# An RK4 scan with two quantized feed-forwards: a searched order of issue, a norm's shift pre-written in PSUM, and merged scale operations

## The chip, the cores and the metric

The kernel runs on one core of one Trainium2 chip, in one launch. The metric is the device time of that launch in microseconds; the time before is 832.3 us, the median of three runs (832.07 to 835.12). The core has five engines that each work through a queue of their own in order: PE (matrix products), DVE, ACT and POOL (elementwise work, called VectorE, ScalarE and GpSimd elsewhere), and SP, which issues DMAs.

## The reference, cut to what matters

The input `x` has 128 sequences of 32 time steps of 256 numbers, `cond` has 128 x 256. Two layers follow each other, each with a first part and a feed-forward (all in float32):

```python
# layer 0, first part: 32 steps of Runge-Kutta 4 over the state (q, p), driven by x[:, t, :]
dq = q - q**3 / 3 - p + drive + tanh(q) @ coupling.T + bias
dp = 0.08 * (q + 0.7 - 0.8 * p)              # four slopes a step, q and p clipped to +-20
# layer 0, feed-forward on the q of every step, with block quantization (blocks of 32):
#   scale = 2**floor(log2(max |block|)), elements rounded to a few bits, clipped
x = x + q_act(silu(q_act(q) @ wg.T) * (q_act(q) @ wu.T)) @ wd.T
# layer 1, first part: modulated norm, then attention with 16 heads over the 32 steps
scale, shift = split(cond @ W_emb + b_emb)
xn = rms_norm(x, g_norm) * (1 + scale) + shift
o = attention(rms_norm(q), rms_norm(k), v)   # qkv = xn @ W_qkv
h = o + o @ W_out
# layer 1, feed-forward: Hadamard rotation, 8-bit rows, ternary weights
x = x + h_bitlinear(silu(h_bitlinear(h, wg)) * h_bitlinear(h, wu), wd)
```

## The kernel before, in words

The batch of 128 lies on the 128 partitions. Stage one goes over the 32 time steps: `step` computes one Runge-Kutta step, and `ffn0` takes the state of that step through layer 0's feed-forward and layer 1's norm and writes the normalized row, turned, into `xnT`. Stage two goes over 32 groups of 128 tokens (4 sequences of 32 steps): `tokens` computes attention and layer 1's feed-forward. The PSUM buffers of the two stages are different, and the first group of stage two waits for all 32 `xnT` copies.

No engine's order is written by hand. Every piece of work is an `Item` given to `Work.add`, with its engine, a cost in microseconds, the buffers that it reads and writes, a rank, and marks such as `port` (the planner lets no two items with that mark run at once on DVE and POOL). `Work.order` simulates the items with these costs, forth and back in time in turn, 40 times, with the priorities taken from the times of the pass before, and keeps the order with the earliest modelled end; stage by stage. The items are then issued in that order, each engine's own part of it as its queue. `keep_warm` adds empty matmuls (L1367) where the plan has gaps on PE.

What the change and the prediction touch:

- `mx_scales` (L679, L684, L691): three DVE instructions on the maxima of the blocks. L679 scales the maxima from an SBUF tile (`amax`) into a small PSUM tile (`top`); L684 and L691 read `top`, cut out the exponent bits as int32, and leave the scale `scl` and its inverse `inv` in SBUF. `ffn0` calls it twice a step: for 8 blocks of the state and for 32 blocks of the inner row. `mx_weight` calls it six times, for the weights; there L736 multiplies `scl` once more, in SBUF.
- Behind these, L922 (DVE) or L970 (POOL) multiplies by `inv`, L902 clips, and L928 or L978 (POOL) multiplies by `scl`. L629 is POOL's multiplication in the four slopes of the Runge-Kutta step, L573 DVE's multiply and add there, L665 its clipping. L740, L752 and L761 are POOL's work on the weights.
- The norm at the end of `ffn0`: L985 (ACT) writes x into `ps_po`, a single PSUM slot, and eight matmuls (L989) add the down product; ACT copies the sum out (L995) and takes its squares (L1001), POOL the inverse root (L1006, L1007). For the first 27 steps ACT scales (L1012) and POOL multiplies by `gain` (L1016) and adds `shift` (L1020); for the last five (`LATE`) DVE does both (L1025, L1027). PE turns the row into a slot of `ps_turn` (L547) and ACT copies it into `xnT` (L1030).
- `modulation` computes `gain` and `shift` once, early.
- In stage two L1253 is two DVE instructions on one element per partition, the scales of gate and up. L1091, L1092 and L1323 are more small scale instructions. L1104 is a DVE instruction on 32 int32 numbers in `rsqrt` (a multiply and an add, SBUF to SBUF) between POOL's instructions L1101 and L1112. L1307 are the butterflies of the rotation, on POOL and DVE, and L1173 POOL's multiplication of the queries by their gains.

Of the kernel before, what the change touches and what calls it, by code (L numbers as in the profile page):

```python
# [13 lines left out]
I32 = mybir.dt.int32  # L14
# [56 lines left out]
class Buf:  # L71


    def __init__(self, slots):
        self.slots, self.slot = slots, None
        self.writers, self.readers, self.left = [], [], 0
        self.end, self.fixed, self.pool = 0.0, False, None
# [6 lines left out]
class Slot:  # L84
    def __init__(self, ap, bank=None):
        self.ap, self.bank, self.free = ap, bank, 0.0


class Item:


    def __init__(self, engine, cost, fn, rank, table, port, tail, records):
        self.engine, self.cost, self.fn, self.rank = engine, cost, fn, rank
        self.table, self.port, self.tail, self.records = table, port, tail, records
        self.after, self.before, self.open = [], [], 0
        self.bufs, self.outs, self.small, self.behind, self.warm = [], (), False, (), None
        self.ready, self.start, self.end = 0.0, None, None


class Work:  # L100

    TAIL = {PE: 0.165, DVE: 0.085, ACT: 0.1, POOL: 0.045, SP: 0.0}
# [7 lines left out]
    ROUNDS = 40  # L112
    GAP, SECOND = 0.45, 100.0

# [3 lines left out]
    def add(  # L118
# [16 lines left out]
        for b in item.bufs:  # L135
            b.left += 1
# [3 lines left out]

    def start_of(self, item, now, port, table):
        t = max(now, item.ready)
        if not self.strict and not all(i in self.gone for i in item.behind):
            return math.inf
        if item.port:
            t = max(t, port)
        for b in item.bufs:
            if b.slots and b.slot is None:
                free = [s.free for s in b.slots if s.free < math.inf]
                if self.strict and b not in b.pool[: len(free)]:  # L150
                    return math.inf
                t = max(t, min(free, default=math.inf))
        if item.table and item.table != table:
            t += self.LOAD
        last = self.last[item.engine]
        if item.engine == PE:
            t = max(t, self.fetched(item.records) - item.cost)
            if last and last.small != item.small:
                t = max(t, now + self.COLD)
        elif item.engine == DVE and last and self.banks(last.outs) & self.banks(item.bufs):  # L160
            t = max(t, now + self.WITHIN[DVE])
        return t

    @staticmethod
    def banks(bufs):
        return {b.slots[b.slot or 0].bank for b in bufs if b.slots} - {None}

    def fetched(self, n):

        n -= self.BLOCK  # L170
        for records, t in reversed(self.issued):
            n += records
            if n > 0:
                return t + self.FETCH
        return 0.0
# [7 lines left out]
    def run(self, items, forth, before):  # L183

        ready = {e: [] for e in (PE, DVE, ACT, POOL, SP)}  # L190
        now = dict.fromkeys(ready, 3.0 if forth else 0.0)
        if forth:
            now[POOL] = 7.0
        port, table = 0.0, None
        self.issued, self.last, self.gone = [], dict.fromkeys(ready), set(before)
        for item in items:
            item.open = 0
            item.ready = 0.0
            for a in item.after if forth else item.before:
                if a in self.gone:  # L200
                    item.ready = max(item.ready, a.end + self.gap(a, item))
                elif (a.rank < self.SECOND) == (item.rank < self.SECOND):
                    item.open += 1
            for b in item.bufs:
                b.left, b.end = 0, 0.0
                if b.slots and not b.fixed:
                    b.slot = None
                for s in b.slots:
                    s.free = 0.0
        if forth:  # L210
            for item in before:
                now[item.engine] = max(now[item.engine], item.end)
                self.last[item.engine] = item
                table = item.table or table
                for b in item.bufs:
                    for s in b.slots:
                        s.free = 0.0
            for item in before:
                for b in item.bufs:
                    if b.slots:  # L220
                        s = b.slots[b.slot]
                        s.free = max(s.free, item.end + item.tail + self.TAIL[item.engine] + 0.06)
        pools = {}
        for item in sorted(items, key=lambda i: i.prio):
            for b in item.bufs:
                if b.slots and b.slot is None and not b.left:
                    b.pool = pools.setdefault(id(b.slots), [])
                    b.pool.append(b)
                b.left += 1
        for item in items:  # L230
            if not item.open:
                ready[item.engine].append(item)
        done = []
        while len(done) < len(items):
            best = None
            for e, waiting in ready.items():
                starts = [(self.start_of(i, now[e], port, table), i) for i in waiting]
                starts = [s for s in starts if s[0] < math.inf]
                if not starts:
                    continue  # L240
                first = min(s[0] for s in starts)
                t, item = min(
                    (s for s in starts if s[0] <= first + 1e-6 + self.LOOK.get(e, 0.0)),
                    key=lambda s: (
                        s[1].prio
                        + self.PRICE * (s[0] - first)
                        + (1.5 if e == ACT and s[0] > first + 1e-6 else 0.0)
                    ),
                )
                if best is None or (t, item.prio) < (best[0], best[1].prio):  # L250
                    best = (t, item)
            assert best is not None, "every item waits for a slot"
            t, item = best
            ready[item.engine].remove(item)
            idle = item.engine == PE and t > now[PE] + 1.5 * self.COLD
            item.start, item.end = t, t + item.cost + (self.COLD if idle else 0.0)
            now[item.engine] = item.end
            self.last[item.engine] = item
            self.gone.add(item)
            if item.engine == PE:  # L260
                self.issued.append((item.records, item.start))
            if item.port:
                port = item.end
            if item.table:
                table = item.table
            for b in item.bufs:
                if b.slots and b.slot is None:
                    b.slot = min(range(len(b.slots)), key=lambda n: b.slots[n].free)
                    b.slots[b.slot].free = math.inf
                    b.pool.remove(b)  # L270
                b.left -= 1
                b.end = max(b.end, item.end + item.tail + self.TAIL[item.engine] + 0.06)
                if b.slots and not b.left:
                    b.slots[b.slot].free = b.end
            done.append(item)
            for i in item.before if forth else item.after:
                if (i.rank < self.SECOND) == (item.rank < self.SECOND):
                    i.ready = max(i.ready, item.end + (self.gap(item, i) if forth else self.gap(i, item)))
                    i.open -= 1
                    if not i.open:  # L280
                        ready[i.engine].append(i)
        return done

    def order(self):
# [4 lines left out]
        for item in self.items:  # L289
            for a in item.after:  # L290
                a.before.append(item)
            for b in item.bufs:
                b.fixed = b.slot is not None
            item.prio = item.rank
        chosen = []
        for second in (False, True):
            items = [item for item in self.items if (item.rank >= self.SECOND) == second]
            best = math.inf
            for n in range(self.ROUNDS):
                self.strict = n > 0  # L300
                done = self.run(items, True, chosen)
                end = max(item.end for item in done)
# [4 lines left out]
                for back in (True, False):  # L307
                    for item in items:
                        item.prio = -item.end
# [3 lines left out]
            for b, slot, end in places:  # L313
                b.slot, b.end = slot, end
# [1115 lines left out]
```

## Time and profile before

| what | value |
|---|---|
| median of three runs | 832.3 us |
| the profiled execution: its time, its span | 832.79 us, 830.6 us |
| PE busy | 774.7 us (93%) |
| DVE busy | 718.7 us (87%) |
| POOL busy | 609.7 us (73%) |
| ACT busy | 504.8 us (61%) |
| mean granted clock of PE | 0.995 |

All times in the prediction are of the profiled execution, counted from the start of its span. A row of a group of instructions reads: line of the kernel, engine, operation, output<-inputs, shapes, count, then the busy time in us with the mean of one in ns, and the idle time of the engine ahead of them with what ended it. A row of a line's instructions gives the smallest, median and largest duration in ns. A row of the timeline gives start and duration in us, with the count of like instructions in it; durations of neighbouring DVE instructions overlap in the records.

### The profile page before, as it was taken

The page shows a single profiled execution, that of the slowest core. Times are in us where ns is not written, and L with a number is a line of the kernel's source. Part 1 is how long each engine was busy: PE and PEld are TensorE (multiplying, and loading weights), DVE is VectorE, ACT ScalarE, POOL GpSimd, SP SyncE. Part 2 cuts the span into 40 slices and gives each one's busy share as a digit, 9 for nine tenths or more (in the row PEclk, how much of TensorE's full clock was granted, in tenths as well). Part 3 has the DMA queues.
Part 4 walks back from the last instruction along what each step waited for, and adds up shares of the span by engine and source line. Part 5 has one row for each costly group of instructions (what it writes and reads, how often), then busy time and mean ns, then how long its engine had stood idle before and what let it go on. Part 6 is the DMA issues. An engine that isn't in the chain of part 4 may idle for free.

```text
span 830.6 us, 25967 instructions
## 1 busy us (share of the span) xinstructions
PE 774.7 (93%) x10357; PEld 571.6 (69%) x10357; DVE 718.7 (87%) x1848; ACT 504.8 (61%) x1021; POOL 609.7 (73%) x956
## 2 busy tenths in 40 slices
PE   6789999999999999998789999999999999999996
PEld 3666677767777677776466576777767686678675
DVE  5899999999999999998368798979798798888794
ACT  3233466655565578685324676768668577765864
POOL 5788899997897898998464677785774878767320
PEclk9999999999999999999999999999999999999999
DMA  7332223332232454342300021234212122221333
GB/s 228 112 46 52 53 69 78 74 71 71 58 75 52 77 146 128 70 115 63 73 2 7 20 52 39 41 71 66 57 38 54 44 52 52 38 63 41 70 83 77
DMA packets 128889, 55.51 MB, mean 67 GB/s; under 512 B 102144, under 2 KB 127616, under 8 KB 128768
## 3 DMA queue, kind: packets, MB, share of 16 engines
q1 hardware_dynamic: 128768, 53.85, 28.4%
q8 instruction: 81, 1.33, 0.7%
q14 instruction: 40, 0.33, 0.1%
HBM read 21.32 MB, written 8.39 MB: 36 GB/s over the span
## 4 chain that ended last, share of the span: by engine, by line
PE 40%; DVE 31%; ACT 10%; POOL 9%; issue 7%; DMA 3%; SPq 0%; ACTq 0%; DVEq 0%; POOLq 0%
PE ps_stage L622 5%; PE ps_stage L608 5%; PE ps_one L1138 5%; PE ps_two L1276 4%; PE ps_two L1318 4%; DVE ps_sum L573 3%; DVE slim L573 3%; DVE tiny L701 3%; DVE tiny L1084 3%; DVE wide L1307 3%; PE ps_one L1220 2%; PE ps_gu L943 2%; PE ps_one L1190 2%; DMA slim_bf<-slim_bf 2%; PE ps_two L547 2%
## 5 line engine op out<-in xcount | busy, mean ns | idle before, releaser
L1307 POOL TENSOR_TENSOR wide<-wide 128x512 f32<-128x512 f32 x116 | 148.1, 1297 | 58.9 <-DVE wide L1307 24.8
L622 PEld LDWEIGHTS ps_stage<-slim,coup 128*128 128x128 f32 x1024 | 129.3, 191 | 19.9 <-ACT slim L615 14.5
L622 PE MATMUL ps_stage<-slim,coup 128*128 128x128 f32 x1024 | 138.5, 278 | 1.3
L629 POOL TENSOR_TENSOR slim<-slim,slim 128x256 f32<-128x256 f32 x96 | 73.0, 760 | 23.7 <-ACT slim L616 19.2
L608 PE MATMUL ps_stage<-slim,eye 128*128 128x256 f32 x256 | 81.9, 401 | 8.3 <-DVE slim L573 7.9
L616 ACT ACTIVATE slim<-slim 128x256 f32<-128x256 f32 x96 | 39.2, 408 | 59.3 <-DVE slim L573 55.4
L978 POOL TENSOR_TENSOR wide_bf<-mid,tiny 128x512 bf16<-128x512 fp8e4 x64 | 67.0, 1050 | 3.6 <-DVE mid L902 3.2
L970 POOL TENSOR_TENSOR mid<-mid,tiny 128x512 f32<-128x512 f32 x64 | 66.6, 1049 | 2.6 <-DVE tiny L691 2.5
L1318 PE MATMUL ps_two<-had_ffn,wide 128*128 128x128 f32 x512 | 63.6, 278 | 1.6 <-ACT wide L1313 1.1
L1318 PEld LDWEIGHTS ps_two<-had_ffn,wide 128*128 128x128 f32 x512 | 60.3, 192 | 5.5 <-ACT wide L1313 2.8
L608 PE MATMUL ps_stage<-drives,eye 128*128 128x256 f32 x192 | 61.9, 405 | 1.6 <-DVE ps_stage L573 0.6
L615 ACT ACTIVATE slim<-slim 128x256 f32<-128x256 f32 x96 | 39.2, 409 | 38.0 <-DVE slim L573 37.4
L1138 PE MATMUL ps_one<-w_qkv_sb,xnT 128*128 128x512 f32 x128 | 61.4, 603 | 0.3 <-ACT v_pad L1154 0.2
L608 PEld LDWEIGHTS ps_stage<-slim,eye 128*128 128x128 f32 x256 | 39.0, 189 | 30.8 <-DVE slim L573 29.4
L1284 ACT ACTIVATE mid<-ps_two,tiny 128x512 f32<-128x512 f32 x64 | 43.4, 687 | 24.4 <-PE ps_two L1276 20.9
L1307 DVE TENSOR_TENSOR wide<-wide 128x512 f32<-128x512 f32 x76 | 56.8, 771 | 1.2 <-POOL wide L1307 1.2
L1220 PEld LDWEIGHTS ps_one<-v_pad,mid 32*32 32x32 f32 x4096 | 41.1, 105 | 23.5 <-issue 18.6
L1291 DVE SCALAR_TENSOR_TENSOR wide<-ps_two,tiny,mid 128x512 f32<-128x512 f32 x64 | 46.9, 741 | 9.1 <-ACT mid L1284 8.3
L1326 ACT ACTIVATE wide<-ps_two,magic,tiny 128x1024 f32<-128x1024 f32 x32 | 38.6, 1205 | 26.3 <-DVE tiny L1092 23.6
L1220 PE MATMUL ps_one<-v_pad,mid 32*32 32x17 f32 x4096 | 47.0, 181 | 4.3 <-issue 2.5
L1084 DVE TENSOR_REDUCE tiny<-ps_two 128x1 f32<-128x1024 f32 x32 | 38.6, 1207 | 9.2 <-PE ps_two L1318 7.6
L902 DVE SCALAR_TENSOR_TENSOR mid<-mid,ps_sum 128x512 fp8e4<-128x512 f32 x64 | 43.2, 680 | 2.3 <-POOL mid L970 2.1
(169 smaller groups left out, 2099.4 us busy)
## 6 DMA issues: line engine op xcount, KB each, us to landing
x_step<-in_x_dram SPq DMA_DIRECT2D x32, 128.0 KB, 2.4
x_add<-in_x_dram SPq DMA_DIRECT2D x32, 128.0 KB, 2.2
x_dram<-slim SPq DMA_DIRECT2D x32, 128.0 KB, 1.9
slim<-x_dram SPq DMA_DIRECT2D x32, 128.0 KB, 2.3
out_dram<-slim SPq DMA_DIRECT2D x32, 128.0 KB, 1.8
raws<-in_L_ffn_w_gate_dram SPq DMA_DIRECT2D x4, 512.0 KB, 5.6
raws<-in_L_ffn_w_up_dram SPq DMA_DIRECT2D x4, 512.0 KB, 6.8
raws<-in_L_ffn_w_down_dram SPq DMA_DIRECT2D x4, 512.0 KB, 3.9
```

Source lines behind the costliest of these rows:

```text
L573: add(DVE, 0.335, lambda: stt(dst.ap, in0.ap, scalar, in1.ap, MULT, op1), reads, [dst], rank=rank)
L608: PE, cost, lambda: nc.tensor.matmul(ps[i].ap, lhsT=eyes[eye], rhs=src.ap, start=False, stop=True, skip_group_check=True),
L622: nc.tensor.matmul(ps[i].ap[:, sl], lhsT=coup[i][:, c, sl], rhs=two(th.ap)[:, c, :], start=False, stop=True, skip_group_check=True,)
L629: POOL, 0.685, lambda: nc.gpsimd.tensor_tensor(sq.ap, sq.ap, qi.ap, MULT),
L970: lambda it=it, ks=ks: nc.gpsimd.tensor_tensor(blocks(it.ap), blocks(it.ap), spread(binv.ap[:, ks], BLOCK), MULT),
L978: lambda b8=b8, ks=ks, sl=sl: nc.gpsimd.tensor_tensor(blocks(bq.ap[:, sl]), blocks(b8.ap), spread(bscl.ap[:, ks], BLOCK), MULT),
L1084: lambda: nc.vector.tensor_reduce(am.ap[:, 0:1], src.ap[:, :n], AX.X, ALU.max, apply_absolute_value=True),
L1138: nc.tensor.matmul(pqk.ap, lhsT=xnT_flat[:, c, tok], rhs=w_qkv_sb[:, c, : 2 * N], start=(c == 0), stop=(c == NC - 1),)
L1220: nc.tensor.matmul(by_v(po.ap)[row, hd, :], lhsT=by_head(exT.ap)[row, hd, :], rhs=v_pad.ap[row, hd, :], start=True, stop=True,)
L1291: lambda pgu=pgu, act=act, sl=sl: stt(it.ap[:, sl], pgu.ap[:, HALF:], sgu.ap[:, 1:2], act.ap, MULT, MULT),
L1307: eng.tensor_tensor(dv[:, :, e, :], sv[:, :, 0, :], sv[:, :, 1, :], op)
L1318: nc.tensor.matmul(pfh.ap[:, sl], lhsT=iT.ap[:, sl], rhs=had_ffn, start=True, stop=True)
```

## The change

Four things change. First, the planner. It is rewritten over lists of numbers with the same costs, it makes 150 passes forth and back, and then `climb` tries 1000 random changes of the priorities:

```diff
-    ROUNDS = 40
+    ROUNDS, TRIALS = 150, 1000
...
+    def climb(self, s, least, found):
+        rng = random.Random(1)
+        prio, limit, first = list(found[1]), math.inf, min(found[1])
+        for _ in range(self.TRIALS):
+            width = 40.0 * rng.uniform(0.3, 1.3)
+            low = rng.uniform(first - width, least)
+            share = 1.0 if rng.random() < 0.5 else 0.15
+            if rng.random() < 0.15:
+                low, width, share = first, least - first, 0.15
+            sigma = rng.expovariate(1.0)
+            trial = [
+                p + rng.gauss(0.0, sigma) if low <= p < low + width and rng.random() < share else p for p in prio
+            ]
+            result = self.run(s, trial, True)
+            if result and max(result[2]) <= limit:
+                prio, limit = trial, max(result[2])
+                if limit <= least:
+                    least, found = limit, result
+        return least, found
```

Second, `ffn0` takes its scales from a new function with two instructions; the weights keep `mx_scales` (with 8.0 for 0.25 in L736):

```diff
+    def block_scales(amax, nb, rank):
+        scl, inv = Buf(tiny), Buf(tiny)
+        bits = lambda b: b.ap[:, :nb].bitcast(I32)
+        add(
+            DVE, 0.1, lambda: nc.vector.tensor_scalar(bits(scl), bits(amax), EXP_MASK, None, ALU.bitwise_and),
+            [amax], [scl], rank=rank,
+        )
+        add(
+            DVE, 0.1,
+            lambda: nc.vector.tensor_scalar(bits(inv), bits(scl), -1.0, float(250 << 23), MULT, ADD),
+            [scl], [inv], rank=rank,
+        )
+        return scl, inv
...
-        scl, inv = mx_scales(am, nb, rank, 32.0, tiny)
+        scl, inv = block_scales(am, nb, rank)
...
-        bscl, binv = mx_scales(bam, FF // BLOCK, rank, 32.0, tiny)
+        bscl, binv = block_scales(bam, FF // BLOCK, rank)
```

Third, the norm's shift. `modulation` computes `shift` turned (features on partitions), with two small products and two ACT instructions for one wide product and a DVE instruction, and loads the shift's bias by itself. `ps_po` becomes twice as wide; ACT copies the turned shift into its second half, and the transpose of the row accumulates onto it. `ps_turn` is no longer used for this, and the shift additions on POOL and DVE go:

```diff
-    ps_po = banks("ps_po", N, 1)
+    ps_po = banks("ps_po", HALF, 1)
...
-            add(
-                POOL, 0.685, lambda: nc.gpsimd.tensor_tensor(xn.ap, xn.ap, shift, ADD),
-                [b_shift], [xn], rank=rank, port=True,
-            )
...
-            add(DVE, 0.335, lambda: tt(xn.ap, xn.ap, shift, ADD), [b_shift], [xn], rank=rank, port=True)
-        add(PE, 0.22, lambda: turn(px.ap, xn.ap), [xn], [px], rank=rank)
+        add(ACT, 0.27, lambda: nc.scalar.copy(two(t_of()), shift), [b_shift], fills=[po], rank=rank)
+        def onto_shift():
+            for c in range(NC):
+                sl = slice(c * P, (c + 1) * P)
+                nc.tensor.matmul(
+                    t_of()[:, sl], lhsT=xn.ap[:, sl], rhs=ident, is_transpose=True,
+                    start=False, stop=True, skip_group_check=True,
+                )
+        add(PE, 0.22, onto_shift, [xn], [po], rank=rank)
         xnT_done.append(
-            add(ACT, 0.4, lambda: nc.scalar.copy(xnT[:, :, :, t], two(px.ap)), [px], fills=[b_xnT], rank=rank)
+            add(ACT, 0.4, lambda: nc.scalar.copy(xnT[:, :, :, t], two(t_of())), [po], fills=[b_xnT], rank=rank)
         )
```

Fourth, in stage two one instruction on two elements per partition takes the place of the two of L1253:

```diff
-        def scales_of_gate_and_up():
-            for n in range(2):
-                ts(sgu.ap[:, n : n + 1], am.ap[:, 0:1], wscale[:, n : n + 1], None, MULT)
-
-        add(DVE, 0.2, scales_of_gate_and_up, [am, b_ws], [sgu], rank=rank)
+        add(
+            DVE, 0.1, lambda: ts(sgu.ap[:, :2], wscale[:, :2], am.ap[:, 0:1], None, MULT), [am, b_ws], [sgu], rank=rank
+        )
```

## The prediction

> **What bounds the kernel now.** The page gives a span of 830.6 us in an execution of 832.79 us (832.3 us is the median of the runs, so 0.5 us less than the execution that I sum against). I read first the busy time by stretches, since the average hides two stages: stage one (the RK4 steps with the first feed-forward) runs to about 412 us, stage two after it.
>
> ```profile
> core 0: us, PE busy (x) PEld busy (x) DVE busy (x) ACT busy (x) POOL busy (x), PEclk, DMA share, GB/s
> 100.00:200.00 100.00, 97.23 (x626) 74.07 (x626) 98.04 (x284) 59.09 (x172) 91.45 (x123) 1.00 0.30 72
> 440.00:760.00 320.00, 310.16 (x6751) 227.73 (x6741) 273.97 (x652) 216.59 (x311) 227.04 (x435) 1.00 0.22 45
> ```
>
> In the middle of stage one DVE is busy 98% and POOL 91%; PE shows 97%, but its matmuls overlap in the records. DVE hardly waits for anybody there, so a microsecond added to DVE's queue in stage one is a microsecond of time, and one taken away is saved. From 385 to 412 us the stage drains: there DVE is busy 16.0 of 27 us, POOL 16.6 and PE 19.9. Stage two is set by PE (97%); DVE has 14% to spare.
>
> Next I read by form which DVE instructions the change touches, from 100 to 350 us, and the POOL instructions of the same stretch.
>
> ```profile
> L679 DVE TENSOR_SCALAR ps_sum<-tiny 128x32 f32<-128x32 f32 x24 | 4.5, 189 | 0.2
> ...
> L679 DVE TENSOR_SCALAR ps_sum<-tiny 128x8 f32<-128x8 f32 x23 | 3.7, 163 | 0.0
> ```
>
> ```profile
> L978 POOL TENSOR_TENSOR wide_bf<-mid,tiny 128x512 bf16<-128x512 fp8e4 x48 | 50.2, 1048 | 2.7 <-DVE mid L902 2.5
> L970 POOL TENSOR_TENSOR mid<-mid,tiny 128x512 f32<-128x512 f32 x48 | 50.1, 1049 | 1.2 <-DVE tiny L691 1.2
> L629 POOL TENSOR_TENSOR slim<-slim,slim 128x256 f32<-128x256 f32 x68 | 49.6, 730 | 12.7 <-ACT slim L616 10.2 <-DVE slim L573 1.0 <-DVE ps_sum L665 0.9
> L1016 POOL TENSOR_TENSOR slim<-slim,gain 128x256 f32<-128x256 f32 x24 | 17.5, 727 | 1.0 <-ACT slim L1012 1.0
> L1020 POOL TENSOR_TENSOR slim<-slim,shift 128x256 f32<-128x256 f32 x23 | 16.7, 728 | 0.3
> L629 POOL TENSOR_TENSOR slim<-slim,states 128x256 f32<-128x256 f32 x22 | 16.0, 729 | 1.4 <-ACT slim L616 1.1 <-DVE ps_stage L573 0.3
> L928 POOL TENSOR_TENSOR slim_bf<-slim,tiny 128x256 bf16<-128x256 fp8e4 x24 | 14.8, 615 | 1.0 <-DVE slim L902 0.6 <-DVE tiny L684 0.2
> L1007 POOL TENSOR_TENSOR tiny<-tiny,neg_half 128x1 f32<-128x1 f32 x24 | 13.4, 557 | 2.0
> ```
>
> What the DVE rows tell is in their operands: L679 writes PSUM and L684 and L691 read it (ps_sum), so all three scale instructions have PSUM on one side. POOL's instructions are long, 0.6 to 1.05 us. So I looked for DVE instructions that are as small but have SBUF on both sides. Line L1104 is one (stage two), a multiply and add on int32, the very form of the change's new `inv`; L1253 is the same kind over one element.
>
> ```profile
> L1104 DVE TENSOR_SCALAR tiny<-tiny x32: 118/182/1253, 416.5 to 749.0; 128x32 int32<-128x32 int32 x32
> ```
>
> ```profile
> L1253 DVE TENSOR_SCALAR tiny<-tiny,wscale x64: 118/203/209, 451.3 to 798.5; 128x1 f32<-128x1 f32 x64
> ```
>
> L1104 takes 182 ns at the median and up to 1253; L1253 never over 209, though 43 of the 64 began while POOL had more than 0.06 us left to run. The timeline shows why, at 465 us and again at 28.6 us (L736, 128x32, SBUF on both sides):
>
> ```profile
> 465.15 1.27 POOL L1307 TENSOR_TENSOR wide<-wide 128x512 f32<-128x512 f32 x1
> 465.37 1.08 DVE L1104 TENSOR_SCALAR tiny<-tiny 128x32 int32<-128x32 int32 x1
> ```
>
> ```profile
> 28.57 0.19 DVE L691 TENSOR_SCALAR tiny<-ps_sum 128x32 int32<-128x32 int32 x1
> 28.68 0.28 DVE L684 TENSOR_SCALAR tiny<-ps_sum 128x32 int32<-128x32 int32 x2
> 28.72 0.72 POOL L629 TENSOR_TENSOR slim<-slim,slim 128x256 f32<-128x256 f32 x1
> 28.89 0.68 DVE L736 TENSOR_SCALAR tiny<-tiny 128x32 f32<-128x32 f32 x2
> 29.40 1.94 POOL L740 TENSOR_TENSOR wide<-raws,tiny 128x1024 f32<-128x1024 f32 x1
> ```
>
> L1104 starts while POOL's L1307 runs to 466.42 and ends 0.03 us after it. L691 and L684 pass under a running POOL instruction at about 0.1 us each, but the first L736 lasts 591 ns, until L629's end at 29.44. The second L736 slipped through in 170 ns although POOL's next instruction was there. So a small DVE instruction with SBUF on both sides is held until POOL's instruction ends.
>
> The Trainium skill, page "SBUF — State Buffer", section "Who interferes with whom", names the rule and speaks against this change: a `tensor_scalar` with source and destination in SBUF may take the port pair that DVE shares with GpSimd, and whichever comes second is blocked for the other's whole instruction. By the rule alone the 128 operations of (b) and the 32 of (e) below would each be held for what POOL has left, an estimated 53 us; by the one row L1104 it would be 23 us.
>
> **The change, part by part.** (a) `block_scales` in place of `mx_scales` in ffn0: two calls a step, 32 steps. It removes 64 instructions (L679) from DVE. They follow each other at 0.1 us for 128x32 (the timeline above) and 0.07 us for 128x8 (their starts in the trace), since durations overlap: 32 x 0.1 + 32 x 0.07 = 5.5 us saved.
>
> (b) The other 128 (L684 and L691 by position) lose their PSUM operand: `scl` and `inv` now read and write tiny tiles in SBUF, and nothing in the planner marks them as users of the shared port. An instruction that comes at a random moment to an engine working in pieces of length d waits on average sum(d x d) / 2 per unit of time. With the POOL rows above over 250 us: 48 x 1.048² + 48 x 1.049² + 68 x 0.73² + 24 x 0.727² + 23 x 0.728² + 22 x 0.729² + 24 x 0.615² + 24 x 0.557² = 195 us², over 500 gives 0.39 us. Without L1020, which goes, 0.37, and with the stage a tenth longer 0.34. The other bound is L1104 itself: from 440 to 760 us its mean is 358 ns against 0.175 unhindered, so 0.18 us, in a stretch where POOL is busy 71% and often waits for L1104. I take 0.28: POOL is fuller here, but a DVE that falls behind leaves POOL idle more often, as `inv` is what L970 waits for. 128 x 0.28 = 36 us; ends 23 and 44. DVE has nothing else to do meanwhile, and behind it on its queue stand the RK4 nests that PE and ACT wait for.
>
> (c) The norm. POOL's shift add goes for 27 steps (27 x 0.73 = 20 us of POOL, off the path); for the last five, DVE's at 0.465 us (L1027), 2.3 us, in the drain where DVE idles 11 of 27 us, so 0.5 us on the chain of the last step and 1 elsewhere: 1.5 saved. ACT gets 32 copies of the shift into PSUM, 0.38 us each by L985: 12 us on an engine busy 59%, in idle time; they would cost at most those 12. Transposing onto PSUM costs PE what the transposes cost before. ps_po, a single slot, is now held until the xnT copy: 0.38 (L985) + 1.72 (eight matmuls) + 0.37 + 0.57 + 0.75 (rsqrt) + 0.47 + 0.73 + 0.45 + 0.60 = 6.0 us and some 0.6 of hand-overs, against a step of 11.2 us (22 steps in 247 us). It fits; in the drain, where five L1025 come 7.2 us apart, the cover is about 1.3 us.
>
> (d) The modulation runs once: 3 small ACT and PE items in a stretch that waits for weights, and one more 256-element load in SP's queue (0.4 us of issue, about 2 us to land). Nothing on the path; 1 us if that fails.
>
> (e) One scale instruction (128x2) for two (128x1) in stage two: 32 x 0.12 = 3.8 us less on DVE. Whether two elements are held like L1104 or pass like L1253 no row shows: between 0 and 32 x 0.29 (what POOL still had to run at L1253's starts) = 9 us more. DVE is not the bound there, so I count +1, with ends -2 and +5. The Trainium skill, page "VectorE: DVE Perf Modes", section "Mode 2×_2P — use both read ports for one tensor", asks for an even size of the outermost dimension that isn't one: by it two elements would be held, and (e) would be at its upper end, +5.
>
> (f) The order. The longer search can win where the plan has slack: 2 to 4% of idle DVE in stage one, the 27 us drain, 3% of PE in stage two and its two ends. No row prices it; all idle DVE of 40 to 385 us is 12 us, the drain perhaps 5, stage two's idle PE 10 us. I take 6 saved, with ends of 0 and 18; the plan that it improves doesn't know of the waits in (b), so part of it is lost.
>
> Sum: 832.8 + 36 - 5.5 - 1.5 + 1 - 6 = 856.8; less the 0.5 to the median, 856 us.
>
> **The rivals.** Faster: the new order puts most `scl` and `inv` where POOL stands still, or 8 elements pass like one. The waits decide against the change from a mean of (5.5 + 1.5 + 6 - 1) / 128 = 0.09 us an instruction; below that it is faster, and with next to none 832.3 - 12 = 820 us, down to 812 with a better order. For it: 21 of 32 L1104 take no more than 183 ns. Against it: POOL is busy 91%, and the planner sees no reason to avoid it. Chance 0.16.
>
> The second of a pair slips through like the second L736: then 64 x 0.34 = 22 us instead of 36, 842 us. Chance 0.22.
>
> The second always meets POOL's next instruction in full: 64 x 0.34 + 64 x 0.75 = 70 us, 890, or some 875 with POOL idling more. Chance 0.12. The held ps_po serializes the drain, adding 5 us or more (861 and up): chance 0.05.
>
> **How the numbers follow.** The forecast case, 843 to 868 us, has 0.45. The range 826 to 880 leaves out most of the first rival (0.14) and the top of the third (0.05). About 0.5%, 4 us, is what a measurement of this kernel can tell from no change: faster 0.16, same 0.06 (the low end of the second rival with a good order), slower 0.78.
>
> **What would show it.** Right: in stage one the new lines of `block_scales` show means of 0.35 to 0.5 us with maxima near 1.1, ending just after POOL's instructions; DVE stays at 97%; POOL falls to some 80%; stage two begins at 435 to 445 us and lasts 415 to 420. Wrong: means under 0.2 us there with POOL running, or stage one no longer than 412 us; a stage two shorter by over 10 us would mean that I priced the search too low.

## The result, and the profile after

The changed kernel takes 844.36 us at the median (844.03 to 844.59) beside 833.71 us for the kernel before on the same chip: a ratio of 1.0125, 95% interval 1.0094 to 1.0156. That is slower by 10.7 us, where I had forecast 24.

The profiled execution has a span of 842.3 us. Its busy times by stretches, for the two that were shown of before (columns as there):

```profile
100.00:200.00 100.00, 94.00 (x594) 70.72 (x594) 98.59 (x252) 60.43 (x176) 84.39 (x114) 1.00 0.31 70
440.00:760.00 320.00, 306.21 (x6765) 224.69 (x6764) 282.81 (x640) 218.84 (x311) 233.55 (x457) 1.00 0.21 43
```

In the middle of stage one DVE is as full as before (98.6% for 98.0%) but gets through 252 instructions in 100 us where it got through 284, more than the removed ones explain; POOL falls from 91 to 84%, most of it because L1020 is gone (16.7 us of 250 before). The instructions that take the block scales, by form from 100 to 350 us, before:

```profile
L691 DVE TENSOR_SCALAR tiny<-ps_sum 128x32 int32<-128x32 int32 x24 | 4.5, 186 | 0.2
L684 DVE TENSOR_SCALAR tiny<-ps_sum 128x32 int32<-128x32 int32 x24 | 4.4, 183 | 0.0
...
L691 DVE TENSOR_SCALAR tiny<-ps_sum 128x8 int32<-128x8 int32 x23 | 3.6, 157 | 0.1
L684 DVE TENSOR_SCALAR tiny<-ps_sum 128x8 int32<-128x8 int32 x23 | 3.6, 156 | 0.0
```

and those of `block_scales` after (L826 gives `scl`, L831 gives `inv`):

```profile
L831 DVE TENSOR_SCALAR tiny<-tiny 128x8 int32<-128x8 int32 x22 | 10.5, 477 | 0.0
...
L826 DVE TENSOR_SCALAR tiny<-tiny 128x32 int32<-128x32 int32 x24 | 7.9, 328 | 0.1
L826 DVE TENSOR_SCALAR tiny<-tiny 128x8 int32<-128x8 int32 x22 | 6.8, 310 | 0.0
L831 DVE TENSOR_SCALAR tiny<-tiny 128x32 int32<-128x32 int32 x24 | 6.4, 266 | 0.2
```

Their means are 266 to 477 ns where L679, L684 and L691 took 156 to 189. The timeline shows one that is held and one that is not, both beside POOL's L1131 (the first multiplication behind `inv`, L970 before):

```profile
121.78 1.05 POOL L1131 TENSOR_TENSOR mid<-mid,tiny 128x512 f32<-128x512 f32 x1
121.81 1.04 DVE L831 TENSOR_SCALAR tiny<-tiny 128x8 int32<-128x8 int32 x1
```

```profile
302.33 0.16 DVE L826 TENSOR_SCALAR tiny<-tiny 128x8 int32<-128x8 int32 x1
302.35 1.05 POOL L1131 TENSOR_TENSOR mid<-mid,tiny 128x512 f32<-128x512 f32 x1
```

The first starts 0.03 us behind POOL's instruction and ends at 122.85, 0.02 us after it. The second starts 0.02 us ahead of POOL's and is done in its usual time. Of the 128, 53 last more than 195 ns; every one of these ends 0.02 to 0.04 us after the POOL instruction that ran beside it. The other 75 take 153 to 182 ns, like L684 and L691 before.

Where the time went is read from the chain of work at the seam of the stages (columns: start, length, what). The first product of stage two, that of the queries and keys, is L1138 before and L1305 after:

```profile
412.54 0.04 issue
412.59 0.49 PE ps_one L1367 x3
413.07 3.44 PE ps_one L1138 x8
```

and after:

```profile
429.27 0.60 ACT xnT L1197
429.87 0.04 issue
429.91 0.80 PE ps_one L1532 x3
430.71 2.62 PE ps_one L1305 x4
```

Below, "stage one" is the start of the first record of that product on PE (412.9 us before, 430.5 after), and "stage two" the rest of the span. So stage one is 17.6 us longer and stage two 5.9 us shorter (417.7 to 411.8).

### The profile page after: what moved, and what is told of

Its sections match the earlier page's. It is cut to its first block, busy times and chain, and to the rows that moved or that the text cites. A ratio compares the mean times of both kernels' runs of the same rounds, so it can differ in the third digit from the quotient of the medians.

```text
span 842.3 us, 25714 instructions
## 1 busy us (share of the span) xinstructions
PE 763.7 (91%) x10275; PEld 566.6 (67%) x10275; DVE 738.9 (88%) x1746; ACT 520.4 (62%) x1057; POOL 596.8 (71%) x929
## 4 chain that ended last, share of the span: by engine, by line
DVE 43%; PE 33%; issue 8%; ACT 7%; POOL 6%; DMA 3%; SPq 0%; DVEq 0%; ACTq 0%; POOLq 0%
DVE ps_sum L696 4%; DVE slim L696 4%; PE ps_stage L745 4%; PE ps_two L1441 4%; PE ps_two L1483 4%; PE ps_one L1305 3%; DVE tiny L839 3%; PE ps_stage L731 3%; DVE ps_stage L696 3%; DVE wide L1472 3%; DVE mid L1063 2%; PE ps_one L1387 2%; DVE mid L1116 2%; DVE tiny L1251 2%; PE ps_one L1312 2%
## 5 line engine op out<-in xcount | busy, mean ns | idle before, releaser
L1472 POOL TENSOR_TENSOR wide<-wide 128x512 f32<-128x512 f32 x116 | 151.0, 1321 | 51.8 <-DVE wide L1456 20.3
L1131 POOL TENSOR_TENSOR mid<-mid,tiny 128x512 f32<-128x512 f32 x64 | 66.4, 1049 | 13.2 <-DVE tiny L831 9.0
L1305 PE MATMUL ps_one<-w_qkv_sb,xnT 128*128 128x512 f32 x128 | 61.5, 608 | 1.1 <-ACT slim L1424 0.9
```

The lines of the kernel that those rows point to most:

```text
L1131: lambda it=it, ks=ks: nc.gpsimd.tensor_tensor(blocks(it.ap), blocks(it.ap), spread(binv.ap[:, ks], BLOCK), MULT),
L1305: nc.tensor.matmul(pqk.ap, lhsT=xnT_flat[:, c, tok], rhs=w_qkv_sb[:, c, : 2 * N], start=(c == 0), stop=(c == NC - 1),)
L1472: eng.tensor_tensor(dv[:, :, e, :], sv[:, :, 0, :], sv[:, :, 1, :], op)
```

## The experiments

All ratios are to the kernel before, run beside each on the same chip (its median there was 832.6 to 834.6 us). Except where the order is said to be kept, each kernel has an order of its own, found by the planner.

| kernel | median us | ratio (95%) | stage one | stage two |
|---|---|---|---|---|
| before | 833.71 | 1 | 412.9 | 417.7 |
| the change | 844.36 | 1.0125 (1.0094 to 1.0156) | 430.5 | 411.8 |
| e1, scales through PSUM, its order kept | 835.11 | 1.0006 (0.9990 to 1.0022) | 422.4 | 411.7 |
| e2, two single scales, its order kept | 843.22 | 1.0102 (1.0077 to 1.0126) | 430.6 | 411.1 |
| e3, both | 835.61 | 1.0001 (0.9984 to 1.0018) | 421.4 | 412.5 |
| e4, the merge of block scales alone, order of before kept | 850.95 | 1.0197 (1.0164 to 1.0229) | 428.5 | 420.4 |
| e5, the longer search alone | 827.10 | 0.9913 (0.9901 to 0.9926) | 412.5 | 414.3 |
| e6, all but the longer search | 852.79 | 1.0217 (1.0203 to 1.0230) | 429.6 | 420.0 |
| e7, e5 with the new norm | 829.56 | 0.9947 (0.9929 to 0.9964) | 416.4 | 415.6 |
| e8, planner told of the port | 834.87 | 1.0005 (0.9987 to 1.0022) | 420.8 | 412.2 |
| e9, e7 with two sums in flight | 853.95 | 1.0249 (1.0225 to 1.0272) | 440.8 | 416.6 |
| e10, e5 with the longer hold | 834.19 | 1.0017 (0.9997 to 1.0036) | 418.7 | 413.5 |
| e11, e5 told of older waits | 832.03 | 0.9989 (0.9969 to 1.0009) | 420.9 | 413.5 |
| e12, e13, sister orders of e5 (old norm) | 827.60, 838.19 | 0.9905, 1.0030 | 418.6, 419.4 | 412.6, 414.2 |
| e14, e15, sister orders of e7 (new norm) | 824.65, 825.38 | 0.9881, 0.9881 | 412.6, 412.6 | 410.2, 410.5 |

The intervals of the last two rows are 0.9877 to 0.9933 and 1.0008 to 1.0053, 0.9855 to 0.9907 and 0.9855 to 0.9906. The stages come from one profiled execution each, which can lie a few us from the median (e12's span is 831.1 us).

**e1.** The changed kernel with its own order and buffers; the block scales are emitted as before:

```diff
-        nc.vector.tensor_scalar(bits(scl), bits(amax), EXP_MASK, None, ALU.bitwise_and)
+        nc.vector.tensor_scalar(top, amax.ap[:, :nb], TINY, 32.0, ALU.max, MULT)   # top in PSUM
+        nc.vector.tensor_scalar(bits(scl), top.bitcast(I32), EXP_MASK, None, ALU.bitwise_and)
...
-        nc.vector.tensor_scalar(bits(inv), bits(scl), -1.0, float(250 << 23), MULT, ADD)
+        nc.vector.tensor_scalar(bits(inv), top.bitcast(I32), EXP_MASK, EXP_MASK, ALU.bitwise_and, ALU.bitwise_xor)
```

> The order of issue, the buffers and everything else are those of the changed kernel; only the emission of the block scales in ffn0 goes back to three instructions through a small PSUM tile (64 DVE instructions more, 128 that no longer have SBUF on both sides). Theory A, the wait for POOL: in the changed kernel the 128 instructions last 26 us longer than 175 ns each; that goes, 64 x 0.07 to 0.1 = 5.5 us come back. Stage two begins near 410 us instead of 430.5, and the time is 844.4 - 20 = 824 us (820 to 830). Theory B, the new order and the longer held ps_po delay stage one and the waits lie beside other work: stage two still begins near 430 us, time 844 to 850.

The groups by form from 100 to 350 us show the waits gone:

```profile
L849 DVE TENSOR_SCALAR tiny<-ps_sum 128x32 int32<-128x32 int32 x24 | 4.6, 191 | 0.8
...
L854 DVE TENSOR_SCALAR tiny<-ps_sum 128x8 int32<-128x8 int32 x23 | 3.6, 156 | 0.0
```

The time falls by 9.2 us and stage one by 8.1, not by 20. So the waits are real and on the path, but of 25.9 us of them (what the 128 instructions last over 175 ns) 8.1 + 5.5 = 13.6 came through in this order, if the pitch of the 64 instructions that came back counts in full; and stage one stays 9.5 us longer than before without them. The measured time lies between the two theories. As a whole, undoing this one merge takes away the change's loss: 1.0006, with 1 inside the interval.

**e2, e3.** The merged scale of stage two, undone in the order of the change, alone and with e1:

```diff
-        ts(sgu.ap[:, :2], wscale[:, :2], am.ap[:, 0:1], None, MULT)
+        for n in range(2):
+            ts(sgu.ap[:, n : n + 1], am.ap[:, 0:1], wscale[:, n : n + 1], None, MULT)
```

> The changed kernel in its own order; only the merged scale of gate and up (128x2) is emitted as two instructions on one element again (32 DVE instructions more). Theory A: the 128x2 form waits for POOL (10.9 us over 175 ns each in the changed kernel), the 128x1 form doesn't; 3.8 us come back as pitch; DVE has slack in stage two, so 2 to 7 us fewer: 837 to 842 us, stage one unchanged. Theory B, DVE's slack in stage two hides it all: 844 to 846 us.

> The changed kernel in its own order with both of the above: block scales through PSUM and two single scales. Theory A: the two add up, stage one ends near 410 us and stage two lasts 405 to 410 us: 815 to 822 us, faster than the kernel before (833.7) by its better order of stage two. Theory B: 844 to 852 us.

In the changed kernel the line reads:

```profile
L1419 DVE TENSOR_SCALAR tiny<-wscale,tiny x32: 127/254/1235, 463.2 to 809.9; 128x2 f32<-128x2 f32 x32
```

Two elements are held like 32; one element (L1253) never was. These 32 last 10.9 us over 175 ns. Taking them away brings nothing that can be told from zero: e2 lies within the change's interval, e3 within e1's. So DVE's slack in stage two covers them, as theory B of e2 has it (843.2 us, for its 844 to 846). e3's forecast of 815 to 822 us failed with e1's.

**e4.** The kernel before, its order and buffers kept, with the first of the three scale instructions left out in ffn0 and the other two on SBUF:

```diff
-        nc.vector.tensor_scalar(a(), amax.ap[:, :nb], TINY, mul, ALU.max, MULT)
-        a = lambda: top.ap[:, :nb]      # PSUM
+        a = lambda: amax.ap[:, :nb]     # SBUF; scl and inv read it
```

> The kernel before with its own order and buffers; only in ffn0 the first of the three scale instructions is left out and the other two read the maxima in SBUF (so 64 fewer, and 128 with SBUF on both sides; the inverse scales come out in another scale, which changes numbers and no durations). Theory A: 128 waits of 0.2 us on average, 26 us, less 5.5 us: 850 to 856 us, stage two begins 18 to 22 us later. Theory B, the waits lie beside other work and the fewer instructions save: 828 to 833 us.

```profile
L704 DVE TENSOR_SCALAR tiny<-tiny 128x32 int32<-128x32 int32 x23 | 9.8, 426 | 0.0
L711 DVE TENSOR_SCALAR tiny<-tiny 128x8 int32<-128x8 int32 x23 | 9.4, 407 | 0.0
L711 DVE TENSOR_SCALAR tiny<-tiny 128x32 int32<-128x32 int32 x23 | 8.1, 351 | 0.1
L704 DVE TENSOR_SCALAR tiny<-tiny 128x8 int32<-128x8 int32 x23 | 5.9, 256 | 0.0
```

The same instructions (L684 and L691 before, 156 to 186 ns) now take 256 to 426 ns, and the kernel is 16.3 us slower; stage one is 15.6 us longer. With the 5.5 us of pitch saved by the left-out ones, 21 of 23.9 us of waits came through. This is the cleanest price of the merge: one thing changed, and it alone makes the kernel slower than the whole change did. It also rules out that the instructions are long because `inv` now waits for `scl`: here both read the maxima, as both read `top` before.

**e5, e6, e7.** e5 is the kernel before with the change's planner; e6 the change with the passes and trials of before; e7 the change with `mx_scales` in ffn0 and two single scales, that is search and norm:

```diff
 e6: -    ROUNDS, TRIALS = 150, 1000
     +    ROUNDS, TRIALS = 40, 0
 e7: -        scl, inv = block_scales(am, nb, rank)
     +        scl, inv = mx_scales(am, nb, rank, 32.0, tiny)
```

> The kernel before with nothing changed but the order of issue, found by the longer search. In e3 (no waits of small scales left) stage one still ends at 421.4 us against 412.9 before, and stage two lasts 412.5 against 417.7. Theory N: the norm's held ps_po costs those 8.5 us, so here stage one ends at 411 to 414 us and the time is 825 to 829 us. Theory S: the searched order costs them, because it packs DVE and POOL closer at the weights (start-up) where the chip is not as the plan has it; then stage one ends at 418 to 422 us and the time is 832 to 836 us. Both: stage two 410 to 413 us.

> All of the change but the longer search (40 passes and no random trials). The waits stay: theory A has stage one at 425 to 435 us, with 20 to 28 us over 175 ns in the 128 block scales, and stage two at 416 to 421 us (the old order's 417.7): 843 to 852 us. If the search and not the merge is what costs stage one (theory S of e5), stage one ends at 418 to 424 us.

> The changed kernel with the old block scales (three instructions through PSUM) and two single scales, and its own search over these: the longer search and the norm's shift in PSUM together. Theory N: as e3, 832 to 836 us, stage one at 419 to 423 us. Theory S: the same time, so e5 tells them apart; if both are wrong and e3's stage one was an accident of keeping an order found for other costs, stage one ends at 410 to 414 us and the time is 822 to 827 us.

The order of the longer search gains 7.3 us by itself (e5, as theory N), and taking it from the change loses as much: 1.0217 - 1.0125 = 0.0092, 7.7 us. So the two merges and the norm cost 18 us with the order of the shorter search (e6, in stage one as its theory A), and this order hides 7 to 8 of them. Each of these is the price of one order; e12 to e15 show how far orders scatter. The random trials have no part in this: with 150 passes and no trials the planner gives the same order, item for item, for e5, e7 and the change; the further passes found it. e7 is 2.5 us behind e5 and lies between its theories. e3, the same work as e7 in the change's order, ends stage one 5 us later; that its order was found for other instructions is the likely reason.

**e8.** The new small instructions get `port=True`, so that the plan keeps them out of POOL's:

> The changed kernel with the block scales and the merged scale marked as users of the shared port, so that the search keeps them out of POOL's instructions; nothing else. Theory A: the waits become partly planned: the excess over 175 ns falls from 26 us to 8 to 18 us, but DVE or POOL stands idle for it instead, 832 to 842 us. If marking suffices to hide them, 822 to 830 us.

The excess over 175 ns falls from 25.9 to 9.0 us, and the time to that of the kernel before, within theory A. Of these 17 us 9.7 arrive as a shorter stage one. Against the saving stand DVE's idle time from 20 us to the last RK4 step (19.6 us for 13.3 in the change) and the drain, from the last RK4 step to the end of stage one (33 us for 27).

**e9, e10, e11.** Does the norm's longer hold of ps_po cost the difference of e5 and e7? e9 gives the sum a second place, in the unused halves of the two banks of the slopes; e10 lets the planner count the old norm's ps_po as held until the xnT copy; e11 marks L1104, L736 and L782 as users of the port.

```diff
 e9:  +    second.y, second.t = (tile[:, N:] for tile in stage_tiles)
      +    ps_po.append(second)
 e10: -        add(PE, 0.22, lambda: turn(px.ap, xn.ap), [xn], [px], rank=rank)
      +        add(PE, 0.22, lambda: turn(px.ap, xn.ap), [xn, po], [px], rank=rank)
 e11: -            [v], [y], rank=rank,
      +            [v], [y], rank=rank, port=True,
```

> e7 (longer search, the norm's shift in PSUM, no small scales with SBUF on both sides) with a second place for the down product and the turned row, made of the unused halves of the two PSUM banks of the slopes, and a search of its own. e7 ended stage one at 416.4 us against 412.5 in e5, which has the old norm. Theory N, the longer held ps_po: with two places stage one ends at 410 to 413 us, total 824 to 828 us. Rival, the shift's extra work on ACT or the order cost those 4 us: stage one stays at 415 to 418 us, total 828 to 832 us.

> e5 (the kernel before, longer search) with one difference for the planner: ps_po counts as in use until the row has been copied into xnT, as the change has it; no instruction is added or removed, the new order alone keeps the next step's sum out. Theory N: stage one ends 3 to 6 us later than e5's 412.5 us, total 829 to 833 us. Rival (the hold costs nothing): 826 to 828 us.

> e5 with the planner told that the small instructions that the kernel before already has with SBUF on both sides (L1104 in stage two, L736 and L782 in stage one) use the shared port. L1104 held 5.6 us over 175 ns in the kernel before and 6.8 in e5. If the holds fall on the path and the marking moves them, 2 to 5 us faster than e5: 822 to 825 us. If DVE's slack in stage two covers them, or the marking costs as much order as it saves, 826 to 831 us.

e9 answers nothing: a new cost drowned it. Of DVE's groups from 120 to 400 us, the nests that read the slopes wait 14.3 us, 2.3 in e7 (second row). In e9 3.9 us of it end with the slopes' own products (L769), 3.5 with the products in the other half of their bank (L1175) and 1.4 with ACT's work on it (L1187):

```profile
L720 DVE SCALAR_TENSOR_TENSOR slim<-ps_stage,slim 128x256 f32<-128x256 f32 x69 | 29.0, 421 | 14.3 <-PE ps_stage L769 3.9 <-PE ps_stage L1175 3.5 <-ACT slim L1187 1.4
```

```profile
L712 DVE SCALAR_TENSOR_TENSOR slim<-ps_stage,slim 128x256 f32<-128x256 f32 x72 | 29.9, 416 | 2.3 <-PE ps_stage L761 2.1
```

e10 goes the way of theory N, a little further than its ranges (stage one 6.2 us later, 834.2 us in all). But e11, whose marks hardly touch stage one, ends it 8.4 us later than e5 as well and misses both its ranges, though its L1104 are no longer held (mean 197 ns for 377 in e5). That made the reading of e10, and of e5 against e7, doubtful.

**e12 to e15.** So I asked how far two orders lie apart that the planner holds for about equal: the work of e5 and of e7, each planned with a look-ahead on PE of 0.31 and 0.33 us for 0.30 (and no random trials, which changed nothing in e5 and e7). By the planner's own times stage one of e5, e12 and e13 ends within 0.7 us, and that of e7, e14 and e15 within 0.9.

> The work of e5 (kernel before, old norm) in a sister order: 150 passes with PE's look-ahead at 0.31 for 0.30 us. Theory N (the norm's hold sets the difference of e5 and e7): stage one ends at 411 to 414 us as in e5, total 825 to 830 us. Theory R (orders scatter): anywhere from 412 to 421 us, total 826 to 836 us.

> As e12 with a look-ahead of 0.33 us. Theory N: stage one at 411 to 414 us. Theory R: 412 to 421 us, and differing from e12 and e5 by 3 us or more.

> The work of e7 (shift pre-written in PSUM, block scales through PSUM, two single scales) in a sister order, look-ahead 0.31 us. Theory N: stage one at 416 to 420 us as in e7, above both sisters with the old norm. Theory R: 411 to 421 us, overlapping them.

> As e14 with a look-ahead of 0.33 us. Theory N: stage one at 416 to 420 us. Theory R: 411 to 421 us, overlapping e12 and e13.

Theory R holds, and e13's time lies even above the range that e12 gives for it: the old norm gives 0.9913, 0.9905 and 1.0030, the new one 0.9947, 0.9881 and 0.9881. The groups overlap, and the best orders have the new norm. e14, at 824.65 us, beats both kernels: the longer search and the shift in PSUM, without either merge.

## Why the prediction was right and wrong, point by point

**The mechanism of (b) held, its size did not; that is the step that failed.** I took 0.28 us of waiting for each of 128 instructions, 36 us. The trace has 25.9 us over 175 ns, 0.20 each; and I let every microsecond of it count, where 21 of 23.9 arrived in the order of before (e4) and 13.6 of 25.9 in the change's (e1). The low end, L1104's 0.18, was the nearer row: by it the wait is 23 us and my sum 843 us. That it meets the result so well is partly luck, since not all of the wait arrived. What was wrong in the other bound is the random moment. Of the 128 in the changed kernel, 53 (41%) found POOL standing still, while POOL is busy 81% of 45 to 400 us, which would leave 19%. The groups of POOL from 100 to 350 us say why:

```profile
L1131 POOL TENSOR_TENSOR mid<-mid,tiny 128x512 f32<-128x512 f32 x48 | 49.9, 1050 | 8.5 <-DVE tiny L831 4.4 <-DVE tiny L826 3.7
```

POOL's idle time ahead of L1131 is ended by these very instructions (8.1 of 8.5 us; the like row of before, L970, has 1.2): it stands still because it waits for them. For 36 of the 53, POOL's next instruction was released by one of the small ones. Another 22 passed beside a running POOL instruction: 11 that began almost together with it, 6 at its end, and 5 under L1169. The other 53 were held, 0.5 us each on average. That POOL waits for them I had named ("`inv` is what L970 waits for") and given too little weight.

**The skill's rule.** "SBUF — State Buffer", section "Who interferes with whom", holds here for 2, 8 and 32 elements. The measurement adds that not all of the small instructions meet the case: held were 53 of 128 in stage one. The 53 us that I derived from it for all of them were one and a half times what they lasted over 175 ns (25.9 + 10.9 = 36.8 us), and two and a half to four times what reached the end (21 in e4, 13.6 by e1).

**(a)** was used in each reckoning above and not measured by itself. **(c)** I had a gain of 1.5; e5 and e7 gave a loss of 2.5 and the sisters a gain of a few us. The price of the norm is below the scatter of orders and stays open. That the held ps_po makes the drain 5 us longer (a rival) did not come true: the drain takes 27.0 us in the changed kernel, 27.7 before. I had the transposes onto PSUM cost what they cost before; on the chain at the end of the drain the two take 0.70 us (L1190) where they took 0.45 (L547), and why was not looked into. **(e)** was right in what counts: a hold of 9 us at most was forecast, 10.9 came, and none of it reaches the end. Two elements are held, as the condition of an even size says in the page "VectorE: DVE Perf Modes", section "Mode 2×_2P — use both read ports for one tensor". **(f)** 6 us were counted and 7.3 to 7.7 came, in e5 from further passes and not from random moves. Part of that is luck: of three orders of the same work with 150 passes, e5 and e12 gain 7 to 8 us and e13 loses 2.5.

With measured terms: 16.3 (e4, waits less pitch) - 7.3 (e5) = 9.0, against 10.7; the 1.7 us left over are not assigned, for the terms come from different orders. In the change's own order the merge of block scales costs 9.2 (e1), and the rest is 1.5. With my terms it was 36 - 5.5 - 1.5 + 1 - 6 = 24: of the 13 us between, 14 are the waits (30.5 with the pitch for 16.3).

**The rivals.** The rival that the new order would put the small instructions where POOL stands still was half true: 41% found it so, not enough. "The second of a pair slips through" gave 842 us, next to the result, for a wrong reason: the second instructions (L831) were held nearly as often as the first (24 and 29 of 64), so its nearness is luck.

**What I said would show it.** Means of 0.35 to 0.5 us: 0.27 to 0.48, with maxima of 1.9 and 1.6 us where I had 1.1. POOL at some 80%: 84% from 100 to 200 us, 79% from 200 to 300. Stage two at 435 to 445 us: 430.5. Stage two lasting 415 to 420: 411.8.

Open is why the same waits come through by nine tenths in the order of before (e4) and by about half in the change's order (e1), and why orders that the planner holds for equal end stage one up to 7 us apart.

## What to carry to other kernels

An operand in PSUM on a small VectorE instruction can be worth more than a merged instruction: leaving out 64 of 0.07 to 0.1 us made 128 others wait 0.2 us on average for GpSimd. When two engines exclude each other, don't price the waits from a random moment: look whether the one stands still because it waits for the other, and take a like row of the trace over a formula. Before a change of a few us is credited to its cause in a kernel whose order is searched, measure some sister orders: here they differed by 1.3% with the same work.

## What the runs showed of the hardware that I had not expected

- Which of the two engines waits is decided by which begins first, to about 0.02 us. Counted are the small VectorE instructions of the changed kernel and of e4 whose start in the records lies near that of a GpSimd instruction of over 0.4 us. Of those that start 0.01 to 0.1 us ahead of it 23 of 24 passed; of those that start 0.02 to 0.13 us behind it 22 of 23 were held; in between 14 passed and 11 were held. Left out are the 5 that came under L1169 and the 13 under its like in e4 (L1027), a power on one element per partition: none of these was held.
- A hold depends on the number of elements in this way, for a `tensor_scalar`: 128x1 never (L1253, at most 209 ns), 128x2 up to 1235 ns, 128x8 up to 1862 ns, the last behind POOL's work on a weight tile. With two tensors as inputs one element is enough: L782 of the kernel before (128x1) took 517 to 1000 ns, each time ending 0.02 us after a POOL instruction.
- In e9 two chains of work share a PSUM bank without sharing a number, and DVE stood idle 39 us from 20 us to the last RK4 step, against 21 us in e7. Whether the chip, the program's semaphores or the new order is the cause was not separated.
